# The first triangle stage of an attention-and-triangle kernel, written as a list of words over four steps and three blocks of fronts

## The chip, the cores and the metric

The kernel runs on one core of a Trainium2 chip. The metric is the device time of one execution in microseconds. Five executions of the kernel before gave a median of 3811.55 us, from 3808.18 to 3817.82. All arithmetic is in float32.

## What is computed

The input `x` has four images of 64 x 64 tokens with 256 channels. Two layers follow each other.

```python
# layer 0: attention over the 4096 tokens of an image
f = xt @ Wf + bf; g = xt @ Wg + bg; v = xt @ Wh + bh      # 32, 32 and 128 channels
beta = softmax(einsum('bqd,bkd->bqk', g, f), axis=-1)
x = x + (einsum('bqk,bkd->bqd', beta, v) @ Wo + bo)

# layer 1: triangle attention on the 64 x 64 grid, 8 heads of 32 channels
q, k, v1, v2 = (x @ W for W in (Wq, Wk, Wv1, Wv2))
att = softmax(einsum('bilhd,bljhd->biljh', q, k) / sqrt(32), axis=2)
out = einsum('biljh,bilhd,bljhd->bijhd', att, v1, v2)
h = layer_norm(x + out @ Wo)
y = layer_norm(h + relu(h @ W1 + b1) @ W2 + b2)
```

## The kernel before

**The stages.** For each of the four images there is a stage of layer 0 (attention, about 440 us) and a stage of the triangle product of layer 1 (`first_layer1` for image 0, `next_layer1` for the others). The rest of layer 1 (heads, norms and the two-layer perceptron, class `Tokens`) of image b runs inside the triangle stage of image b + 1, and that of the last image at the end. The triangle stage of image 0 has no such company. In its place it does the *fronts* of images 1 to 3 (class `Ahead`): for each of 24 blocks of 512 tokens it loads the tokens (`load`, the tile `xin`, one buffer of 512 KB), transposes them in two halves on TensorE (`turned`, L315), copies the halves out on ScalarE (`taken`, the tiles `xT`), multiplies them into values (`values`, `vp`) and into attention factors (`factors`, `gf`), and copies and stores all of it to DRAM, to be fetched back by `Ahead.fetch` before image 1's attention.

**One triangle step.** A stage has 32 steps, eight for each of four pairs of heads. A step treats eight rows i.

- `sums` (L758, L760, VectorE): the softmax's row sums of exponentials, and their reciprocals.
- `weights` (L768, ScalarE): eight scaled copies into `es`, two buffers.
- `turn_weights` (L785, TensorE) and `copy_weights` (L793, ScalarE): four transposes into the PSUM tile `att`, and a copy `attP` of the part that GpSimd needs, since it is given SBUF tiles.
- `stationary` (L812, ScalarE): v1 is written into a stationary matrix `wsel`, one for even and one for odd steps.
- `product` (L833): eight products of 128 x 2048 elements, `att` times `v2`. Of step 4i + 3 the last two, of the other steps the last three run on GpSimd (POOL) into `Rp`, which has two buffers; the others on VectorE (DVE) into `R`, three buffers. In four steps that makes 21 products on VectorE and 11 on GpSimd.
- `accumulate` (L843, TensorE): four matmuls for each product into one of the step's two PSUM tiles `acc`.
- `take` (L853, ScalarE), twice in a step: an `acc` is copied into `ao`, two buffers; `store` (L862): eight DMAs to DRAM.

The score blocks of the next pair of heads (`scores`, L731, and their two exponentials in `take_scores`, L741) are spread over the same steps, four blocks for each pair. `acc` and the score blocks share two PSUM buffers (`psA`); `tp`, `vp` and `gf` share two others (`psB`); `att` has two (`psC`). At the changes of pairs the stage loads q and k of the pair after next (`fetch_qk`, tile `qk`, one buffer, four DMAs of 512 KB) and v2 (`fetch_v2`, two buffers, two DMAs of 1 MB). All these loads, the tokens' and all stores of the stage are issued by one queue, SP's, in program order.

**What sets the order.** `run` is under `manual_schedule`: each engine gets its instructions in the order in which the Python code issues them, executes them in that order, and waits at each for the semaphores of what it needs. Before the change, `first_layer1` (L1152) is a loop over steps. The body issues one step's products and accumulates, the next step's `sums`, `weights`, `stationary` and `turn` among them, and in three steps of every four the parts of two blocks of fronts: the values and factors of the block before (`behind`) and the transposes and copies of this step's block (`forward`). `fetches` issues v2's loads at the start of a step, `fetch_qk` likewise; `ahead.load` stands right after the transposes that free `xin`.

`next_layer1` has another form already. A text, `ORDER`, lists words that stand for one piece of work each, and the code goes through the list once for a period of two steps. A number behind a slash says how many periods late a word is executed, so that one pass through the list mixes pieces of neighbouring periods.

Of the kernel before, what the change touches and what calls it, by code (L numbers as in the profile page):

```python
# [41 lines left out]
    r0/1 AO0/2 AO1/2 m1/1 RO4/2 RE5/1 SO/1 RO5/2 TO0/2 sp/1 AO4/2 AO6/2 r1/1 e0/1 e1/1 AO5/2 AE5/1 TO1/2  # L42
    RE4/1 AE4/1 z0/1 WO/1 RE3/1 VO/1 fi/2 SE z1/1 tO/1 so/1 RE6/1 RE0/1 cO/1 sa AE3/1 RE7/1 RE2/1 AE6/1
    AE2/1 AE0/1 rr/1 pp/1 WE RE1/1 AE7/1 AE1/1 fo/1 fa TE1/1 RO2/1 tE TE0/1 RO7/1 h1/-1 RO3/1 h0/-1 ht
    RO6/1 hU AO3/1 hT AO2/1 AO7/1 RO1/1 cE RO0/1 m0 VE
# [4 lines left out]
def attention_then_triangle_kernel(  # L50
# [171 lines left out]
    def factors(ps, xT, t):  # L222
        ps = ps.rearrange("p (w t) -> p w t", w=4)
        for w, wt in enumerate((wg_sb, wf_sb)):
            for cc in range(2):
                for n in range(4):
                    nc.tensor.matmul(
                        ps[32 * n : 32 * n + 32, w, :], wt[:, cc, :], xT[cc][:, ts(n, P)],
                        start=(cc == 0), stop=(cc == 1),
                    )  # L230
        for w, bias in enumerate((bias_g, bias_f)):
            nc.scalar.activation(t[:, w, 0:P], ps[:, w, :], AF.Identity, bias=bias)
# [16 lines left out]
    def front0(b):  # L249
# [22 lines left out]
        for q in range(8):  # L272
# [3 lines left out]
            factors(pb("gf"), [F.yT[cc][:, col] for cc in range(2)], gf)  # L276
# [22 lines left out]
    class Ahead:  # L299
        def __init__(self):  # L300
# [5 lines left out]
            self.n = 8 * (NB - 1)  # L306

# [7 lines left out]
        def turned(self, s):  # L315
            self.tp = []
            for cc in range(2):
                tp = pb("tp")
                for n in range(4):
                    nc.tensor.transpose(tp[:, ts(n, P)], self.x[:, n, ts(cc, P)], ident)  # L320
                self.tp.append(tp)

        def taken(self, s):
            self.xT = []
            for cc, tag in enumerate(("hT", "st")):
                t = work.tile([P, 512], F32, tag=tag, name="xT", bufs=2 + cc)
                self.xT.append(t)
                nc.scalar.copy(t, self.tp[cc])
                nc.sync.dma_start(out=self.d[1 + s // 8]["x"][ts(cc, P), ts(s % 8, 512)], in_=t)


        def values(self, s):
            self.vp = pb("vp")
            for n in range(4):
                for cc in range(2):
                    nc.tensor.matmul(
                        self.vp[:, ts(n, P)], self.xT[cc][:, ts(n, P)], wh_sb[:, cc, :],
                        start=(cc == 0), stop=(cc == 1),
                    )

        def valued(self, s):
            t = work.tile([P, 4, P], F32, tag="s4", name="va")
            nc.scalar.copy(t, self.vp.rearrange("p (n d) -> p n d", n=4))
            nc.sync.dma_start(out=self.d[1 + s // 8]["v"][:, s % 8 * 4 : s % 8 * 4 + 4, :], in_=t)

        def factors(self, s):
            t = work.tile([P, 2, C], F32, tag="h", name="gf", bufs=1)
            factors(pb("gf"), self.xT, t)
# [785 lines left out]
    def fetches(L, step):  # L1134
        pair, ig = divmod(step, NIG)
        L.fetch_v1(step + 2)
        if step == 2:
            L.fetch_v2(1)
        if ig == 0 and 0 < pair < NPAIR - 1:
            L.fetch_v2(pair + 1)  # L1140

    def first_layer1(L, ahead, F):
        b = 0
        ahead.load(0)
        waiting = behind = None
        for step in range(NSTEP):
            pair, ig = divmod(step, NIG)
            more = step + 1 < NSTEP  # L1150
            forward = step // 4 * 3 + step % 4 if step % 4 < 3 else None
            L.begin(step)  # L1152
            ahead.fetch(F, b + 1, step)
            k = L.npool(step)
            D_, Q_ = list(range(8 - k)), list(range(8 - k, 8))
            scored = step % 2 == 1 and pair + 1 < NPAIR
            if scored:
                L.take_scores()
            if step > 0:
                L.take(step - 1, 1)  # L1160
                L.store(step - 1)
            fetches(L, step)
            if scored and ig == 7 and pair + 2 < NPAIR:
                L.fetch_qk(pair + 2)

            late = scored and ig == NIG - 1

            def next_weights():
                if more:
                    L.sums(step + 1)  # L1170
                    L.weights(step + 1)

            L.product(step, Q_[0])
            L.product(step, D_[0])
            L.accumulate(step, D_[0])
            if behind is not None:
                ahead.values(behind)
            if not late:
                next_weights()
            if more:  # L1180
                L.stationary(step + 1)
            L.product(step, Q_[1])
            if behind is not None:
                ahead.valued(behind)
            L.accumulate(step, Q_[0])
            L.product(step, D_[1])
            L.accumulate(step, D_[1])
            if more and not late:
                L.turn(step + 1)
            if behind is not None:  # L1190
                ahead.factors(behind)
            L.product(step, D_[2])
            L.accumulate(step, D_[2])
            if forward is not None:
                ahead.turned(forward)
                ahead.load(forward + 1)
            if late:
                next_weights()
            if k == 3:
                L.product(step, Q_[2])  # L1200
            L.product(step, D_[3])
            L.accumulate(step, D_[3])
            L.take(step, 0)
            if forward is not None:
                ahead.taken(forward)
            behind = forward
            L.accumulate(step, Q_[1])

            if step % 2 == 0 and pair + 1 < NPAIR:
                L.scores(pair + 1, ig // 2)  # L1210
            if more and late:
                L.turn(step + 1)
            L.product(step, D_[4])
            if k == 3:
                L.accumulate(step, Q_[2])
            L.accumulate(step, D_[4])
            if k == 2:
                L.product(step, D_[5])
                L.accumulate(step, D_[5])
        ahead.fetch(F, b + 1, NSTEP)  # L1220
        L.take(NSTEP - 1, 1)
        L.store(NSTEP - 1)


    def next_layer1(b, L, rest, ahead, F):
        own = b == NB - 1
        t0 = NP * (b - 1)


        n2, n1, n0 = NP, NP + own, NP + 2 * own  # L1230
        made, added, taken, stored, held = {}, {}, {}, set(), []
        mv, rs, rn, mps, sps = {}, {}, {}, {}, {}

        def fetched(step):
            if F is not None and 24 <= step < 31:
                ahead.fetch(F, b + 1, step)
            if step == 2:
                L.fetch_v2(1)
            if step in (NIG, 2 * NIG):
                L.fetch_v2(step // NIG + 1)  # L1240


        def load(q, far=False):
            if q < NP or 24 + (q - NP) // 2 in stored:
                rest.load(t0 + q, far)
            else:
                held.append((q, far))

        def store(step):
            L.store(step)  # L1250
            stored.add(step)
            if own and step == 26:
                held.extend((NP + q, True) for q in (2, 3, 4))
            todo, held[:] = list(held), []
            for q, far in todo:
                load(q, far)

        def moments(q):
            if q not in mv:
                mv[q] = small.tile([P, 4, 2], F32, tag="mv", name="mv")  # L1260
            rest.mv = mv[q]

        def scores(j):
            L.scores(1 + j // 4, j % 4)
            sps[j] = L.sp
            if j % 4 == 3 and j // 4 + 2 < NPAIR:
                L.fetch_qk(j // 4 + 2)

        def of_step(word, i):
            step = 2 * i + "EO".index(word[1])  # L1270
            if not 0 <= step < NSTEP:
                return
            w = word[0]
            if w == "R":
# [3 lines left out]
                L.product(step, int(word[2]))  # L1278
                made[step] += 1
                if made[step] == 8:  # L1280
                    fetched(step + 1)
            elif w == "A":
                L.accumulate(step, int(word[2]))
            elif w == "T":
                L.take(step, int(word[2]))
                taken[step] = taken.get(step, 0) + 1
                if taken[step] == 2:
                    store(step)
# [11 lines left out]
            elif w == "c":  # L1300
                L.copy_weights(step)

# [54 lines left out]
        L.fetch_v1(2)  # L1357
        mps[1] = {}
        words = [(w.split("/") + ["0"])[:2] for w in ORDER]
        for period in range(NP + 4):  # L1360
            for word, late in words:
                i = period - int(late)
# [86 lines left out]
```

## Time and profile before

| | us |
|---|---|
| Median of five executions | 3811.55 |
| The profiled execution | 3809.94 |
| its span, from first to last instruction | 3808.1 |
| its first triangle stage, first to last product | 487.8 to 923.4 |
| 88 products on GpSimd in it, median of one | 4.588 |
| 168 products on VectorE in it, median of one | 2.280 |

In the profile, PE is TensorE, PEld its weight loads, DVE VectorE, ACT ScalarE, POOL GpSimd, and SPq the queue that issues DMAs. A row of the view by stretches gives, for each engine, the busy time in the stretch and the number of its instructions, then the TensorE clock that was granted (1 is full), the busy share of the DMA engines, and what they moved. A row of the timeline gives start, busy time, engine, line, operation, tiles written and read, and in brackets the idle time of the engine before it, with what ended that idle time. A matmul in float32 shows as two records, so an accumulate of four matmuls shows as eight. In the rows on DMA the last number is the median time from issue to landing.

### The profile page before, as it was taken

The numbers are of one execution on the slowest core, as the hardware profiler recorded it, in microseconds if no ns is written. First come the engines' busy times: TensorE is split into PE (matmuls) and PEld (weight loads), VectorE is DVE, ScalarE is ACT, GpSimd is POOL, SyncE is SP. The second block draws the span as 40 slices with busy tenths as digits, with TensorE's granted clock in tenths as the row PEclk, the third lists the DMA queues.
The fourth block names the chain that finished last, engine by engine and source line by source line (L and its number), as shares of the span: only waits on it lengthen the run. The fifth ranks groups of instructions, "written<-read, shape, count | busy, mean of one in ns | idle before, by whom it ended". The sixth has DMA issues, their size and how long they took to land.

```text
span 3808.1 us, 60145 instructions
## 1 busy us (share of the span) xinstructions
PE 3677.2 (97%) x23498; PEld 1795.3 (47%) x23498; DVE 2641.0 (69%) x2050; ACT 1934.1 (51%) x4257; POOL 1804.3 (47%) x930
## 2 busy tenths in 40 slices
PE   9999988888999999999999999999999999999997
PEld 5444444433444455554344445555344445555476
DVE  4444488897544459999544448999754455999976
ACT  3333355554333357776333346766533335677654
POOL 4000088896000049999100008999600004999954
PEclk9999999999999999999999999999999999999999
DMA  4111355544111164323111153343211116431221
GB/s 118 54 50 50 99 139 140 149 114 151 36 47 53 50 152 92 89 54 94 62 49 48 52 126 89 79 95 70 92 42 47 50 59 144 95 88 48 69 62 51
DMA packets 439750, 309.43 MB, mean 81 GB/s; under 512 B 299361, under 2 KB 404577, under 8 KB 432161
## 3 DMA queue, kind: packets, MB, share of 16 engines
q1 hardware_dynamic: 419952, 291.12, 29.0%
q10 hardware_dynamic: 16240, 8.59, 0.9%
q0 software_dynamic: 3264, 5.78, 0.6%
q8 instruction: 188, 3.08, 0.3%
q14 instruction: 106, 0.86, 0.1%
HBM read 165.88 MB, written 139.46 MB: 80 GB/s over the span
## 4 chain that ended last, share of the span: by engine, by line
PE 81%; POOL 7%; issue 3%; DVE 3%; DMA 3%; ACT 3%; SPq 0%; ACTq 0%; POOLq 0%; DVEq 0%
PE o L453 24%; PE acc L843 16%; PE proj L510 8%; PE s L431 7%; POOL Rp L833 6%; PE mp L1026 5%; PE zp L1046 5%; PE sp L731 3%; PE v1p L535 3%; PE hp L902 2%; PE y L495 1%; DVE R L833 1%; PE att L785 1%; ACT S L741 1%; PE den L470 1%
## 5 line engine op out<-in xcount | busy, mean ns | idle before, releaser
L833 POOL TENSOR_TENSOR Rp<-attP,v 128x2048 f32<-128x2048 f32 x328 | 1490.1, 4577 | 457.6 <-ACT attP L793 383.8
L833 DVE TENSOR_TENSOR R<-att,v 128x2048 f32<-128x2048 f32 x696 | 1548.4, 2273 | 109.0 <-PE acc L843 74.0
L460 DVE TENSOR_TENSOR esum<-esum,e 128x2048 f32<-128x2048 f32 x224 | 512.7, 2289 | 584.6 <-ACT e L442 581.5
L843 PE MATMUL acc<-R,wsel 128*32 128x512 f32 x5568 | 706.9, 602 | 42.4 <-DVE R L833 29.0
L442 ACT ACTIVATE e<-s 128x1024 f32<-128x1024 f32 x512 | 496.6, 1021 | 404.8 <-PE s L431 387.3
L954 POOL TENSOR_SCALAR nt<-mv 128x4 f32<-128x4 f32 (+1 forms) x51 | 9.8, 193 | 1283.2 <-DVE mv L919 1279.3
L453 PE MATMUL o<-e,vlo 128*128 128x512 f32 x1024 | 475.4, 607 | 0.0
L453 PE MATMUL o<-e,vhi 128*128 128x512 f32 x1024 | 472.6, 605 | 0.0
L853 ACT COPY ao<-acc 128x1024 f32<-128x1024 f32 x256 | 255.3, 1021 | 225.8 <-PE acc L843 196.6
L843 PE MATMUL acc<-Rp,wsel 128*32 128x512 f32 x2624 | 344.1, 598 | 23.8 <-POOL Rp L833 23.6
L843 PEld LDWEIGHTS acc<-R,wsel 128*32 128x32 f32 x5568 | 153.2, 110 | 377.5 <-issue 260.0
L453 PEld LDWEIGHTS o<-e,vlo 128*128 128x128 f32 x1024 | 184.6, 190 | 281.9 <-issue 281.9
L453 PEld LDWEIGHTS o<-e,vhi 128*128 128x128 f32 x1024 | 184.3, 189 | 279.6 <-issue 279.6
L431 PE MATMUL s<-gT,fT 32*128 32x512 f32 x2048 | 302.3, 640 | 4.3 <-ACT e L442 4.0
L768 ACT ACTIVATE es<-S,rd 128x64 f32<-128x64 f32 x1024 | 257.7, 335 | 11.0 <-DVE rd L760 7.7
L472 DVE RECIPROCAL rec<-den 128x512 f32<-128x512 f32 x32 | 107.4, 3357 | 215.6 <-PE den L470 215.6
L1046 PE MATMUL zp<-w,hid 128*128 128x256 f32 x1024 | 247.6, 387 | 7.2 <-ACT hid L1035 7.2
L1026 PE MATMUL mp<-hT,w 128*128 128x256 f32 x1024 | 249.5, 389 | 0.7 <-ACT hT L998 0.7
L1026 PEld LDWEIGHTS mp<-hT,w 128*128 128x128 f32 x1024 | 186.6, 190 | 101.4 <-ACT attP L793 36.0
L1046 PEld LDWEIGHTS zp<-w,hid 128*128 128x128 f32 x1024 | 186.4, 191 | 71.9 <-issue 31.9
L522 ACT COPY st<-proj 128x512 f32<-128x512 f32 x104 | 60.9, 585 | 293.2 <-issue 165.9
L843 PEld LDWEIGHTS acc<-Rp,wsel 128*32 128x32 f32 x2624 | 80.7, 110 | 212.4 <-issue 138.7
(166 smaller groups left out, 3820.7 us busy)
## 6 DMA issues: line engine op xcount, KB each, us to landing
v<-v2d SPq DMA_DIRECT2D x24, 1024.0 KB, 12.9
v1c<-v1d SPq DMA_DIRECT2D x128, 128.0 KB, 2.7
aT<-ao SPq DMA_DIRECT2D x1024, 16.0 KB, 1.9
A<-aT SPq DMA_DIRECT2D x256, 64.0 KB, 2.0
out_dram<-z SPq DMA_DIRECT2D x63, 256.0 KB, 2.5
y<-yT SPq DMA_DIRECT2D x56, 256.0 KB, 2.1
q<-st SPq DMA_DIRECT2D x56, 256.0 KB, 2.6
v1d<-st SPq DMA_DIRECT2D x56, 256.0 KB, 2.2
```

Source lines behind the costliest of these rows:

```text
L431: nc.tensor.matmul(s_ps[r // 2][:, r % 2, :], fT[rows, tt, ts(n, P)], gT[rows, ts(qb, QB)], start=True, stop=not safe,)
L442: nc.scalar.activation(e[g][:, 2 * j : 2 * j + 2, :], s_ps[j], AF.Exp)
L453: nc.tensor.matmul(o_ps[qb], F.v[tt][:, r * 4 + n, :], es[:, r, :], start=(k == 0 and r == 0), stop=(k == 7 and r == 3),)
L460: nc.vector.tensor_tensor(esum[qb], esum[qb], es, ALU.add)
L510: nc.tensor.matmul(ps, w[:, cc, rows], y(qb, cc), start=(cc == 0), stop=(cc == 1))
L535: nc.tensor.matmul(ps[:, ts(n, C)], y(qb, cc)[:, ts(m * 2 + n, P)], wv1_sb[:, cc, :], start=(cc == 0), stop=(cc == 1),)
L768: nc.scalar.mul(e[:, i, :], rows[:, i, :], rec[:, i : i + 1])
L833: eng.tensor_tensor(R, src.unsqueeze(1).to_broadcast([P, D, N]), v2[:, h], ALU.mult)
L843: nc.tensor.matmul(acc[32 * c : 32 * c + 32, n % 2, :], w[:, n, c, 16 * h : 16 * h + 32], R[:, ts(c, 8), :].rearrange("p d j -> p (d j)"), ...
L853: nc.scalar.copy(self.ao[step][:, ts(np, 2)].rearrange("p k d j -> p k (d j)"), self.acc[step][np])
L1026: nc.tensor.matmul(self.mp[:, fc % 2, :], w1_sb[:, cc, ts(fc, P)], self.hT[tt][:, cc, :], start=(cc == 0), stop=(cc == 1),)
L1046: nc.tensor.matmul(zp[:, n, :], self.hid[tt][:, fc, ts(n, P)], w2_sb[:, fc, :], start=(fc == 0), stop=(fc == 3 and tt not in self.hT2),)
```

## The change

The loop over steps is replaced by a second list of words, `ORDER0`, for a period of four steps and three blocks of fronts. The words of a step are now shared by both lists (`step_words`), so `ORDER`'s words have new names in the same order: the letter E or O, for an even or odd step, becomes 0 or 1. In `ORDER0` a word is a letter, a step (0 to 3) or block (0 to 2) of the period, and for some a last digit.

- `R23` is product 3 of step 2, `A23` its accumulate, `T20` and `T21` its two takes; after the second take the step is stored.
- `S`, `W`, `V`, `t`, `c` are sums, weights, stationary (and the load of v1 two steps on), transposes of the weights, and the copy `attP`.
- `sp0` and `sp1` are blocks of scores, `e01`, `e00`, `e11`, `e10` their exponentials by halves. The fourth block of a pair is followed by `fetch_qk` at once, if a pair is left to load.
- `P01`, `P00` are the transposes of block 0's halves 1 and 0, `C01`, `C00` their copies and stores; after a block's second `P` the next block's tokens are loaded.
- `v`, `u` are values and their copy and store; `g`, `a` are factors and their copy (bias) and store.
- `/1` is one period late, `/-1` one early.

`fetch_v2` is now issued when the eighth product of step 1, 7 or 15 has been issued. `Ahead.turned` and `Ahead.taken` do one half at a time, and factors and their bias are two functions, so that other words can stand between.

```diff
+ORDER0 = """
+    A22/1 t3/1 R23/1 V3/1 W0 A26/1 A21/1 g2/1 A23/1 A25/1 R24/1 T20/1 sp1/1 A24/1 S2 S3 c3/1 t0 R27/1
+    v1/1 R31/1 R33/1 a2/1 A27/1 e11/1 e10/1 R30/1 A33/1 A31/1 R32/1 v2/1 u1/1 R37/1 P01 T21/1 A37/1
+    A30/1 C01 S1 R35/1 c0 R36/1 A32/1 R34/1 P00 A35/1 A36/1 C00 g0 V0 R01 A34/1 u2/1 T30/1 R00 W1 R05
+    T31/1 A05 R06 v0 A00 A01 V1 R03 R02 A03 t1 a0 c1 R04 u0 A06 R13 P11 R07 P10 A02 A07 R15 W2 R12 A04
+    T00 C11 T01 sp0 R16 t2 e01 R10 c2 A12 P21 e00 R11 C10 S0/-1 A15 W3 A13 A16 C21 P20 A10 R17 R14 V2
+    A11 A14 A17 R26 g1 R25 R20 T11 T10 a1 R22 R21 A20 C20
+""".split()
...
-        def turned(self, s):
-            self.tp = []
-            for cc in range(2):
-                tp = pb("tp")
-                for n in range(4):
-                    nc.tensor.transpose(tp[:, ts(n, P)], self.x[:, n, ts(cc, P)], ident)
-                self.tp.append(tp)
+        def turned(self, s, cc):
+            tp = self.tp[s, cc] = pb("tp")
+            for n in range(4):
+                nc.tensor.transpose(tp[:, ts(n, P)], self.x[:, n, ts(cc, P)], ident)
...
+    def step_words(L, fetched, stored):
+        made, taken, sps = {}, {}, {}
+
+        def do(w, step, m):
             if not 0 <= step < NSTEP:
                 return
             if w == "R":
                 if step not in made:
                     made[step] = 0
                     L.begin(step)
-                L.product(step, int(word[2]))
+                L.product(step, m)
                 made[step] += 1
                 if made[step] == 8:
+                    if step == 1:
+                        L.fetch_v2(1)
+                    if step in (NIG - 1, 2 * NIG - 1):
+                        L.fetch_v2((step + 1) // NIG + 1)
                     fetched(step + 1)
...
+        def scores(j):
+            if j == 1:
+                scores(0)
+                L.take_scores()
+            if 0 <= j < 12:
+                L.scores(1 + j // 4, j % 4)
+                sps[j] = L.sp
+                if j % 4 == 3 and j // 4 + 2 < NPAIR:
+                    L.fetch_qk(j // 4 + 2)
...
+        def front_word(w, s, cc):
+            if not 0 <= s < ahead.n:
+                return
+            if w == "P":
+                ahead.turned(s, cc)
+                turned[s] = turned.get(s, 0) + 1
+                if turned[s] == 2:
+                    ahead.load(s + 1)
+                    if s + 1 == ahead.n:
+                        ahead.fetch(F, 1, 31)
...
+        for period in range(NSTEP // 4 + 3):
+            for word, late in words_of(ORDER0):
+                i, last = period - late, int(word[-1])
+                if word[0:2] == "sp":
+                    if i >= 0:
+                        scores(2 * i + 1 + last)
+                elif word[0] == "e":
+                    if i >= 0:
+                        take_scores(2 * i + 1 + int(word[1]), last)
+                elif word[0] in "RATSWVtc":
+                    step_word(word[0], 4 * i + int(word[1]), last)
+                else:
+                    front_word(word[0], 3 * i + int(word[1]), last)
```

## The prediction

> **What bounds the kernel now.** I read the page first (TensorE busy for 97% of the span), then the busy times in stretches, because the change touches one stage only: the first triangle stage, from its first product at 487.8 us to its last at 923.4.
>
> ```profile
> core 0: us, PE busy (x) PEld busy (x) DVE busy (x) ACT busy (x) POOL busy (x), PEclk, DMA share, GB/s
> 487.84:921.20 433.36, 381.29 (x4263) 175.47 (x4262) 394.60 (x230) 236.81 (x614) 399.32 (x88) 0.98 0.51 140
> ```
> ```profile
> 518.02:570.53 52.51, 48.15 (x572) 22.58 (x568) 49.63 (x30) 31.04 (x81) 49.99 (x12) 1.00 0.53 143
> 570.53:629.94 59.41, 50.14 (x572) 23.57 (x568) 50.85 (x31) 31.00 (x81) 49.88 (x11) 0.94 0.65 163
> 629.94:682.52 52.58, 48.15 (x572) 22.55 (x568) 48.63 (x29) 30.98 (x80) 49.94 (x12) 1.00 0.36 104
> ...
> 820.86:870.74 49.88, 41.64 (x424) 18.57 (x420) 47.43 (x28) 26.29 (x74) 49.88 (x12) 1.00 0.55 141
> ```
>
> A row is one period of four steps (11 POOL and 21 DVE products). POOL does 399.3 us of work in 433.4; a period needs at least 49.88 on POOL (last row: 11 products without a gap, 4.53 each) and 21 x 2.19 + 4 x 0.83 = 49.3 on DVE (five products and a pair of sums end to end take 11.78, from 876.10 to 887.88). It takes 52.5 undisturbed and 59.4 and 59.8 twice. So the stage is bound by the two product engines, and only their idle time can be won. Next, POOL's own order of time:
>
> ```profile
> 503.23 13.65 POOL L833 TENSOR_TENSOR Rp<-attP,v 128x2048 f32<-128x2048 f32 x3 [1.85 <-PE acc L843]
> 518.02 36.34 POOL L833 TENSOR_TENSOR Rp<-attP,v 128x2048 f32<-128x2048 f32 x8 [1.15 <-PE acc L843]
> ...
> 596.46 27.17 POOL L833 TENSOR_TENSOR Rp<-attP,v 128x2048 f32<-128x2048 f32 x6 [3.22 <-PE att L785]
> 629.94 36.27 POOL L833 TENSOR_TENSOR Rp<-attP,v 128x2048 f32<-128x2048 f32 x8 [6.31 <-ACT ao L853]
> ...
> 820.86 63.46 POOL L833 TENSOR_TENSOR Rp<-attP,v 128x2048 f32<-128x2048 f32 x14 [3.19 <-PE att L785]
> ```
>
> The bracket is the idle time. All of them sum to 34.0: start 1.85 + 1.15; around 600-630 3.22 + 6.31, and the same again (3.26 + 6.67) around 710-742; 3.19 at 820.86; the other seven 8.4. Last, what ended the long ones:
>
> ```profile
> 624.91 1.94 PE L320 MATMUL tp<-ident,xin 128*128 128x128 f32 x8 [4.96 <-DMA xin<-in_x_dram]
> ...
> 626.78 1.94 PE L843 MATMUL acc<-R,wsel 128*32 128x512 f32 x8
> ```
> ```profile
> 611.34 1.42 SPq L311 DMA_DIRECT2D xin<-in_x_dram  x1
> ```
> ```profile
> xin<-in_x_dram SPq DMA_DIRECT2D x21, 512.0 KB, 4.1
> v<-v2d SPq DMA_DIRECT2D x6, 1024.0 KB, 10.8
> ```
>
> A tokens' load lands 4.1 us after its issue; issued behind the two 1 MB loads of v2 (610.1) it took 13.4, and PE, which works in order, stood 4.96 us, then ran slowly (eight transposes 1.94 instead of 1.02, one accumulate 1.71 start to start instead of 0.87).
>
> **The change part by part.** Engine by engine the two programs have the same instructions in the same number, and differ in order only within this stage (and in the branch with maxima, which doesn't run). The later triangle stages get the same words under other names: cost zero. So the sum is POOL's and DVE's idle time.
>
> *Taken away.* All 34.0 us of POOL's idle time, and the 2.2 that DVE works on after POOL ends (921.2 to 923.4): 36.2.
>
> *Steady period.* I laid the words of one period end to end, from R23/1, with row durations: DVE product 2.24, sums pair 0.87, POOL product 4.6, accumulate 0.87, block of scores 2.0, turning weights 0.59, half a front's transposes 0.52, values 1.98, factors 0.95, ACT 1.02 (take, half of scores), 2.0 (weights), 1.0 (wsel). PE has 32 x 0.87 + 2 x 2.0 + 4 x 0.59 + 3 x (1.04 + 1.98 + 0.95) = 46.1 of 50; ACT 31; SP's issues 4 x (5.0 + 0.6) + 3 x 2.45 = 29.8. Each buffer is met in time: R32 starts at 13.0 and waits for A33, done at 11.6; R12 at 34.0 for A02 (31.5). The tightest are POOL's, with two buffers: R05 must not start before A37 ends (15.9), which puts R27 2.1 to 2.6 us after R23, and nothing contradicts it. So a period near POOL's 49.9 fits. Ends: 0 idle, and 2.65 (the period stays 52.55). I take 0.5, nearest to the next stage, already driven by such words, where the limiting PE is busy 27.76 of 27.76 us per two steps. Six periods with scores: 3.0.
>
> *The qk loads.* Issued after the fourth block of scores (sp0 in periods 1 and 3), now behind the load of tokens needed next, and 24 us ahead of the following one; cover 24 against 7.4 to 9 us of landing: zero. Without that cover they would do what v2 does.
>
> *The v2 loads.* R34/1 completes a step and issues the next pair's v2; the buffer's last reader is R34 itself, so SP waits to 20.6 in the period. P00, the next word, issues the tokens that P11 needs. They go out at 21.8, land 13.4 later, 35.2; P11 stands on PE at 30.1. **This wait stays**: 5.1 us. Behind P11: P10 (both 1.94, slow), A02 (1.7), and R12 on DVE waits for A02's buffer until 38.8 instead of 34.0; then sp0, t2 and A12 (44.2), for whose buffer R11 is 5.8 late; A15 frees POOL's R17 6.6 late. I take 6 a time, 12 for two. Ends: 0 (tokens land in the 9.5 us from P00 to P11), and 7.2 (59.8 less 52.6, today's price).
>
> The Trainium skill ("TensorE: Matmul & The Clock Gate", Part 1) has the array at half clock after an idle window of about 3.4 us, for about as long again. By it the slow phase would cost up to 1.7 us a time, against about 2.0 from the rows above; the sum would be 0.6 lower.
>
> *Start.* Before, the first accumulates wait for products only. Now P01, P00 and g0 stand ahead of A05 on PE. Their tokens are issued at 482.98; a transfer issued 0.07 us earlier landed after 10.72, so P01 begins near 493.7. P01 and P00 1.94, copy 0.6, g0 1.9, A05 1.7 (slow clock: 0.83 in 480-500): about 500. R07 on POOL waits for A05's buffer from 497.0: 3.1. A06 now stands behind v0 and three accumulates (506.9), so R15 waits 2.3 more. Sum 5.4, between 3.0 (as before) and 7. Period 0 also does two blocks of scores at sp0, 2.0 on PE ahead of A12: I take 1.0 of it.
>
> *Last two periods.* The loads of gT, vlo and yT (0.5 to 1 MB) are issued at R34 and R07, a word before tokens again: 1.5, between 0 and 5.
>
> *End.* R36 ends POOL's work; R34, DVE's last, ends 4.5 later: 4.5.
>
> New idle: 3.0 + 12 + 5.4 + 1.0 + 1.5 + 4.5 = 27.4. Gain 36.2 - 27.4 = 8.8. The profiled execution took 3809.9 (span 3808.1), so 3801.1; the median of five is 1.6 above it: **3803**.
>
> **The rivals.**
> 1. *The v2 wait is hidden too.* For it: tokens land in 4.1 us without company, and PE has 4 us a period to spare. Against: 13.4 in the same succession. 12 less: 3791.
> 2. *The period stays at 52.5.* For it: R05 has half a microsecond between two constraints, and 33 of DVE's waits (34.2 us) are for accumulates. Against: PE has slack in the walk. 6 x 2.15 = 12.9 more: 3816.
> 3. *Slower: the single gf buffer.* a1 writes it at 47.7 of a period, and a2 may write it again at 4.6 of the next; between them lie eight stores (5.0 us of SP) and gf's own landing, 2.2. ACT's a2 then starts at about 5.0; e11, e10 stand behind it, their buffer holds A33 (10.8), and A33 holds DVE's R32. ACT has 2.8 us in hand. If gf lands more than 2.8 us later than that, each further microsecond is paid in all eight periods. It passes the forecast's gain at 1.1, and is 0.2% slower at 2.1. At 3: 24 more, 3827.
> 4. *The order isn't what the words say.* The instruction order shows it is: 3812, almost no chance.
>
> **How the numbers follow.** About 0.2% (7.6 us, from 3804 to 3819) is what a measurement can tell from no change. Forecast 0.42 (3797 to 3809; 0.27 of it faster, 0.15 within), rival 1 0.25 (faster), rival 2 0.18 (0.15 within, 0.03 slower), rival 3 0.13 (slower), rival 4 0.02 (within). Faster 0.52, within 0.32, slower 0.16. The range takes in rivals 1 and 2: 3787 to 3817; rival 3 and little else is left out.
>
> **What would show it.** Right: POOL in runs of ten products and more, periods of 50 to 51 us except two of about 56, and in these PE waiting some 5 us for xin near P11. Rival 1: no such wait. Rival 2: POOL waits of 1 to 3 us for accumulates in every period. Rival 3: ACT's gf waiting for a DMA (ahg, ahf), and scores' copies late behind it. Wrong altogether if the end of the stage moves by other than the total, or if the later stages change length.

## The result, and the profile after

| | before | after |
|---|---|---|
| Median beside each other, us | 3812.01 (46 runs) | 3809.64 (25 runs) |
| Ratio of the times, 95% interval | | 0.9993 (0.9987 to 0.9998) |
| Profiled execution's span, us | 3808.1 | 3810.0 |
| First triangle stage, first to last product, us | 435.6 | 433.2 |
| POOL's idle time in it, us | 34.0 | 31.2 |
| DVE's work after POOL's end, us | 2.2 | 2.15 |

The change made the kernel 2.4 us faster, 0.07%, which is within the 0.2% called no change. The time lies in the predicted range (3787 to 3817) and 6.6 us above the forecast of 3803. The profiled execution of after is longer than that of before although its stage is shorter: its first triangle product starts at 489.98 instead of 487.84, behind code that did not change. Over all ten profiled executions here this start lies between 487.8 and 490.0, so below the length of the stage is compared, not the time at which it ends. What follows the stage took 2884.7 us before and 2886.8 after (2881.4 to 2889.9 over the ten), so a difference of medians can be some microseconds off the stage's.

The lines of after's program stand 16 further down (the product is L849, the accumulate L859, the transposes of tokens L336). First the row of the stage in the view by stretches:

```profile
core 0: us, PE busy (x) PEld busy (x) DVE busy (x) ACT busy (x) POOL busy (x), PEclk, DMA share, GB/s
489.98:923.17 433.19, 387.12 (x4280) 177.97 (x4278) 392.93 (x224) 234.25 (x615) 399.56 (x88) 0.96 0.52 141
```

POOL's work is nearly the same, 399.6 us against 399.3, so the new length is told by its idle time. POOL's own order of time in after; the bracket is the idle time ahead of a run of products:

```profile
490.02 8.99 POOL L849 TENSOR_TENSOR Rp<-attP,v 128x2048 f32<-128x2048 f32 x2 [327.48 <-ACT attP L809]
503.92 4.55 POOL L849 TENSOR_TENSOR Rp<-attP,v 128x2048 f32<-128x2048 f32 x1 [4.90 <-PE acc L859]
510.39 9.12 POOL L849 TENSOR_TENSOR Rp<-attP,v 128x2048 f32<-128x2048 f32 x2 [1.92 <-PE acc L859]
521.29 27.20 POOL L849 TENSOR_TENSOR Rp<-attP,v 128x2048 f32<-128x2048 f32 x6 [1.79 <-PE acc L859]
551.02 22.76 POOL L849 TENSOR_TENSOR Rp<-attP,v 128x2048 f32<-128x2048 f32 x5 [2.53 <-PE acc L859]
574.24 45.56 POOL L849 TENSOR_TENSOR Rp<-attP,v 128x2048 f32<-128x2048 f32 x10 [0.46 <-PE acc L859]
624.77 4.58 POOL L849 TENSOR_TENSOR Rp<-attP,v 128x2048 f32<-128x2048 f32 x1 [4.97 <-PE acc L859]
631.02 95.43 POOL L849 TENSOR_TENSOR Rp<-attP,v 128x2048 f32<-128x2048 f32 x21 [1.67 <-PE acc L859]
730.84 4.57 POOL L849 TENSOR_TENSOR Rp<-attP,v 128x2048 f32<-128x2048 f32 x1 [4.39 <-PE acc L859]
737.22 99.89 POOL L849 TENSOR_TENSOR Rp<-attP,v 128x2048 f32<-128x2048 f32 x22 [1.82 <-PE acc L859]
839.33 27.21 POOL L849 TENSOR_TENSOR Rp<-attP,v 128x2048 f32<-128x2048 f32 x6 [2.22 <-PE acc L859]
866.90 22.70 POOL L849 TENSOR_TENSOR Rp<-attP,v 128x2048 f32<-128x2048 f32 x5 [0.36 <-PE acc L859]
893.76 27.26 POOL L849 TENSOR_TENSOR Rp<-attP,v 128x2048 f32<-128x2048 f32 x6 [4.17 <-PE acc L859]
```

Two things are to be seen. Left to itself, the list keeps POOL at its limit: 21 products and then 22 without a gap, 95.43 and 99.89 us, 4.54 us each, where before had a gap of 1 us or more after every 3 to 8 products, but for one run of 14 (its gap is 0.59). And all that is left of idle time sits in a few places, each ended "by PE's accumulate", which names the last link only. The link ahead of it is on PE and on SP's queue. Around 620 us in after, SP's issues and then what PE does:

```profile
604.77 1.12 SPq L730 DMA_DIRECT2D v<-v2d  x2
605.98 0.53 SPq L329 DMA_DIRECT2D xin<-in_x_dram  x1
...
612.48 9.96 SPq L878 DMA_DIRECT2D aT<-ao  x8
```
```profile
619.98 1.94 PE L336 MATMUL tp<-ident,xin 128*128 128x128 f32 x8 [5.55 <-DMA xin<-in_x_dram]
621.86 1.87 PE L859 MATMUL acc<-R,wsel 128*32 128x512 f32 x8
623.55 1.03 PE L859 MATMUL acc<-Rp,wsel 128*32 128x512 f32 x8
```

The tokens are issued right behind the two 1 MB loads of v2 and let PE begin 14.0 us later; PE stands 5.55 us with every accumulate queued behind. This is the wait that the prediction said would stay. The next ones it had at zero or small. Around 543 us, ACT, and the stores on SP's queue ahead of it:

```profile
523.90 1.22 SPq L730 DMA_DIRECT2D v<-v2d  x2
...
529.03 10.83 SPq L878 DMA_DIRECT2D aT<-ao  x8
...
540.59 1.08 SPq L366 DMA_DIRECT2D ahf<-gf  x1
```
```profile
542.99 0.37 ACT L247 ACTIVATE gf<-gf,bias_g 128x128 f32<-128x128 f32 x1 [7.13 <-DMA ahf<-gf]
```

Eight stores of a step, 5.0 us of SP in undisturbed steps, take 10.83 behind v2; gf's own stores stand behind them; ACT cannot write the one gf buffer until they have landed. And near the end, where the loads for image 1's attention are mixed in:

```profile
828.84 0.42 SPq L252 DMA_DIRECT2D gT<-ahg  x1
829.36 0.64 SPq L329 DMA_DIRECT2D xin<-in_x_dram  x1
```
```profile
836.20 1.08 PE L336 MATMUL tp<-ident,xin 128*128 128x128 f32 x4 [2.89 <-DMA xin<-in_x_dram]
837.22 1.94 PE L859 MATMUL acc<-Rp,wsel 128*32 128x512 f32 x8
```

With the load of gT issued half a microsecond ahead, PE can begin on the tokens 6.8 us after their issue, where a tokens' load by itself landed after 4.1.

### The profile page after: what moved, and what is told of

Read it like the earlier page. It is cut to its first block, busy times and chain, and to the rows that moved or that the text cites. A ratio compares the mean times of both kernels' runs of the same rounds, so it can differ in the third digit from the quotient of the medians.

```text
span 3810.0 us, 60208 instructions
## 1 busy us (share of the span) xinstructions
PE 3685.2 (97%) x23498; PEld 1798.4 (47%) x23498; DVE 2639.5 (69%) x2050; ACT 1932.3 (51%) x4257; POOL 1805.2 (47%) x930
## 4 chain that ended last, share of the span: by engine, by line
PE 79%; POOL 5%; DVE 4%; DMA 4%; issue 4%; ACT 2%; SPq 1%; ACTq 0%; DVEq 0%; POOLq 0%
PE o L469 24%; PE acc L859 16%; PE proj L526 8%; PE s L447 7%; PE mp L1042 5%; PE zp L1062 5%; POOL Rp L849 4%; PE v1p L551 3%; PE sp L747 3%; DVE R L849 3%; PE hp L918 2%; DMA xin<-in_x_dram 2%; PE y L511 2%; PE att L801 1%; PE den L486 1%
## 5 line engine op out<-in xcount | busy, mean ns | idle before, releaser
L849 POOL TENSOR_TENSOR Rp<-attP,v 128x2048 f32<-128x2048 f32 x328 | 1490.5, 4579 | 456.2 <-ACT attP L809 385.0
L849 DVE TENSOR_TENSOR R<-att,v 128x2048 f32<-128x2048 f32 x696 | 1546.4, 2274 | 107.3 <-PE acc L859 76.0
L859 PE MATMUL acc<-R,wsel 128*32 128x512 f32 x5568 | 705.4, 605 | 33.8 <-DVE R L849 22.9
L859 PE MATMUL acc<-Rp,wsel 128*32 128x512 f32 x2624 | 349.9, 605 | 13.2 <-POOL Rp L849 12.4
L859 PEld LDWEIGHTS acc<-R,wsel 128*32 128x32 f32 x5568 | 153.1, 110 | 366.5 <-issue 267.3
L859 PEld LDWEIGHTS acc<-Rp,wsel 128*32 128x32 f32 x2624 | 80.9, 111 | 202.0 <-issue 139.0
```

The lines of the kernel that those rows point to most:

```text
L849: eng.tensor_tensor(R, src.unsqueeze(1).to_broadcast([P, D, N]), v2[:, h], ALU.mult)
L859: nc.tensor.matmul(acc[32 * c : 32 * c + 32, n % 2, :], w[:, n, c, 16 * h : 16 * h + 32], R[:, ts(c, 8), :].rearrange("p d j -> p (d j)"), ...
```

## The experiments

The theory after this reading (A): the list reaches the limit of the two product engines, and what is left is tokens, and stores, that queue behind larger loads on SP's queue. The rival (B): the list's order itself is at its limit, and a wait that is taken away comes back at the next buffer. The table has all runs; the stage is measured from first to last product, the idle time is POOL's in it, and the fourth column is PE's waiting time for `xin` (in how many waits).

| run | median, us | ratio to before (95%) | stage, us | POOL idle, us | PE for xin, us |
|---|---|---|---|---|---|
| after | 3809.64 | 0.9993 (0.9987 to 0.9998) | 433.2 | 31.2 | 24.2 (8) |
| e1 | 3798.65 | 0.9953 (0.9939 to 0.9967) | 423.6 | 22.1 | 20.4 (8) |
| e2 | 3804.52 | 0.9976 (0.9967 to 0.9986) | 427.6 | 25.9 | 14.5 (7) |
| e3 | 3783.15 | 0.9921 (0.9906 to 0.9936) | 409.3 | 9.6 | 6.3 (1) |
| e4 | 3801.61 | 0.9962 (0.9948 to 0.9975) | 423.7 | 22.0 | none |
| e5 | 3792.31 | 0.9938 (0.9924 to 0.9951) | 410.9 | 10.5 | 13.0 (7) |
| e6 | 3783.40 | 0.9912 (0.9897 to 0.9927) | 404.4 | 3.7 | 5.9 (6) |
| e7 | 3808.00 | 0.9980 (0.9971 to 0.9989) | 424.7 | 23.5 | 18.8 (7) |
| e8 | 3796.88 | 0.9948 (0.9935 to 0.9962) | 417.1 | 15.6 | 16.7 (8) |

e1 to e4 ran on one chip, on which before took 3813.48, and e5 to e8 on another, 3816.31; between the two groups the ratios are compared.

**e1: v2 a step later.** The next pair's v2 is issued behind the eighth product of steps 2, 10 and 18 instead of 1, 7 and 15, in the first triangle stage alone, so that the tokens needed soon go ahead of it.

```diff
-    def step_words(L, fetched, stored):
+    def step_words(L, fetched, stored, v2_at=(1, NIG - 1, 2 * NIG - 1)):
...
-                    if step == 1:
-                        L.fetch_v2(1)
-                    if step in (NIG - 1, 2 * NIG - 1):
-                        L.fetch_v2((step + 1) // NIG + 1)
+                    if step in v2_at:
+                        L.fetch_v2(v2_at.index(step) + 1)
...
-        step_word, scores, take_scores = step_words(L, fetched, lambda step: None)
+        step_word, scores, take_scores = step_words(L, fetched, lambda step: None, (2, 10, 18))
```

> The changed kernel, with the loads of v2 issued when the eighth product of step 2, 10 or 18 has been issued (R24/1, early in a period, after which the next tokens' load is 14 us away) instead of step 1, 7 or 15. Everything else as in the changed kernel. Theory A (the idle time that is left in the stage comes from tokens that queue behind larger loads): the two waits of 5.6 us for xin go, with the 6.6 and 6.2 us of POOL's idle time behind them, and the gf wait of period 1 (2.5 us of POOL) too: 13 to 15 us less than the changed kernel's 3809.6, about 3796. Theory B (the list's order is at its limit, and the wait moves to another buffer): POOL idles elsewhere by as much, 3807 to 3812.

The ratio falls by 0.0040, some 15 us, more than the 9.1 us that POOL's idle time loses and the 9.6 us by which the stage is shorter; the intervals of the two ratios allow for that difference. POOL's idle time of 4.97 + 1.67 and 4.39 + 1.82 us is gone, and so is that of period 1, as these rows of e1's POOL show:

```profile
519.60 49.97 POOL L849 TENSOR_TENSOR Rp<-attP,v 128x2048 f32<-128x2048 f32 x11 [1.76 <-PE acc L859]
569.86 27.23 POOL L849 TENSOR_TENSOR Rp<-attP,v 128x2048 f32<-128x2048 f32 x6 [0.29 <-PE acc L859]
597.66 72.69 POOL L849 TENSOR_TENSOR Rp<-attP,v 128x2048 f32<-128x2048 f32 x16 [0.58 <-ACT attP L809]
671.86 27.22 POOL L849 TENSOR_TENSOR Rp<-attP,v 128x2048 f32<-128x2048 f32 x6 [1.50 <-PE acc L859]
```

A holds for the waits behind v2. Not all of the time was won, though: the gaps of 1.50 us here and of 2.09 at 774 are new. They stand a period later than the old ones, where after had none, behind waits of PE for tokens (2.31 and 2.72 us) that have no large load right ahead of them on the queue. The last two periods lost 1.5 us more than in after.

**e2: v2 after steps 1, 9 and 17.** The same edit with (1, 9, 17). v2 is clear of the tokens here too, but stands ahead of gf's stores.

> The changed kernel, with the loads of v2 issued after the eighth product of step 1, 9 or 17 (R14, late in a period, right after the tokens' load and right ahead of eight stores and of the stores of gf). Theory A with the single gf buffer as a second queue: the token waits go (13 us of POOL), but in each of the two periods after a load ACT waits some 7 us for gf's stores, as it did once in the changed kernel at 536 to 543, and POOL 2.5 to 3 us behind it: 7 to 8 us less than the changed kernel, about 3802. If gf's buffer does not matter: 13 less, 3797. Theory B: no gain, 3810.

PE waits less for tokens than in e1 (14.5 us against 20.4), and yet the kernel is slower than e1. POOL in e2, and ACT ahead of its first long gap:

```profile
653.12 22.76 POOL L849 TENSOR_TENSOR Rp<-attP,v 128x2048 f32<-128x2048 f32 x5 [4.20 <-PE acc L859]
...
758.62 45.47 POOL L849 TENSOR_TENSOR Rp<-attP,v 128x2048 f32<-128x2048 f32 x10 [4.48 <-PE acc L859]
```
```profile
643.47 0.37 ACT L247 ACTIVATE gf<-gf,bias_g 128x128 f32<-128x128 f32 x1 [7.32 <-DMA ahf<-gf]
```

This is the single gf buffer, the mechanism of the prediction's third rival, in the periods in which v2 delays gf's stores. The gaps are larger than the 2.5 to 3 us expected, and the gain is smaller for it.

**e8: e2 with two gf buffers.** One edit to e2, which shows whether that reading is right.

```diff
-            t = work.tile([P, 2, C], F32, tag="h", name="gf", bufs=1)
+            t = work.tile([P, 2, P], F32, tag="gf2", name="gf", bufs=2)
```

> The kernel with v2's loads after steps 1, 9 and 17 (3804.5 in its run, POOL idle 4.20 us at 653 and 4.48 at 759), and the factors' tile gf in two buffers instead of one, nothing else. If the single gf buffer is the mechanism of these two waits (ACT's gf behind the landing of the stores of the gf before, which stand behind v2 on SP's queue), both go, 8 to 9 us, POOL's idle time falls from 25.9 to about 17, and the median is 3795 to 3797. If the wait only passes to the next thing behind the same queue (ao's two buffers, the tokens), POOL still stands 3 to 4 us at each of the two places and the median stays at 3802 to 3805.

POOL in e8, over the same stretch:

```profile
569.35 99.94 POOL L849 TENSOR_TENSOR Rp<-attP,v 128x2048 f32<-128x2048 f32 x22 [0.53 <-PE acc L859]
669.70 77.16 POOL L849 TENSOR_TENSOR Rp<-attP,v 128x2048 f32<-128x2048 f32 x17 [0.42 <-PE acc L859]
```

Both gaps are gone, ACT no longer waits for gf's stores at all, POOL's idle time falls by 10.3 us and the ratio by 0.0028 (10.7 us). The wait did not pass on to the next buffer. The mechanism is shown. The edit also takes gf out of a tag that it shares with a tile of later stages; what follows the stage took 2886.4 us against 2887.2 in e2, so the gain lies in the stage.

**e3: the tokens loaded once.** Only the first block of tokens is loaded; the other 23 loads are left out, and the fronts are computed from the first block's tokens again.

```diff
         def load(self, s):
-            if s < self.n:
+            if s == 0:
```

> The changed kernel with the tokens of the fronts loaded once: the 23 further loads are left out, and all 24 blocks of fronts work on the first block's tokens (so the values and factors of images 1 to 3 are not those of the reference). All other work stays. Theory A: nothing but the first xin wait is left; POOL loses its 12.9 us at the v2 loads and most of the 6.8 us in the last two periods, 15 to 20 us less, 3790 to 3795. Theory B: POOL's waits for accumulates stay, less than 5 us gained.

The stage falls to 409.3 us, and the median is 7 us below the lower end expected. Apart from the start, POOL has one gap of 0.77 us and then works 77 products in one run of 349.42 us. The missing loads (11.5 MB) also took most of POOL's gap behind gf in period 1 (2.53 to 0.77), which the expectation had kept, and all of those in the last two periods. So none of these waits belongs to the order of the list alone: they need the loads. This run takes the loads away altogether; that their places on the queue are what counts is shown by e1, e5 and e6.

**e4: the loop of before, with two of its v2 loads moved.** In the kernel before, the v2 loads of pairs 2 and 3 go out at the start of steps 11 and 19 instead of 8 and 16.

```diff
-        if ig == 0 and 0 < pair < NPAIR - 1:
-            L.fetch_v2(pair + 1)
+        if step in (11, 19):
+            L.fetch_v2(pair + 1)
```

> The kernel before, with no list of words; only the loads of v2 of pairs 2 and 3 are issued at the start of steps 11 and 19 instead of 8 and 16, that is in the one step of four in which no tokens are loaded. Theory A: the two waits for xin of about 5 us, with POOL's 6.3 and 6.7, go there as well; 12 to 14 us less than the kernel before, about 3799, and so more than the list of words itself brought. Theory B (the loop's order is the limit, and the list was needed): less than 4 us.

One moved line in the old loop gives 0.38%, five times what the whole list gave. No wait of PE for `xin` is left in its stage; what remains is put down here to the old order, though ACT still waits 7.0 us there for stores. Rows of e4's POOL:

```profile
597.24 27.20 POOL L833 TENSOR_TENSOR Rp<-attP,v 128x2048 f32<-128x2048 f32 x6 [3.22 <-PE att L785]
624.91 36.30 POOL L833 TENSOR_TENSOR Rp<-attP,v 128x2048 f32<-128x2048 f32 x8 [0.46 <-PE acc L843]
662.71 13.67 POOL L833 TENSOR_TENSOR Rp<-attP,v 128x2048 f32<-128x2048 f32 x3 [1.51 <-PE acc L843]
677.42 22.76 POOL L833 TENSOR_TENSOR Rp<-attP,v 128x2048 f32<-128x2048 f32 x5 [1.04 <-PE acc L843]
703.43 27.21 POOL L833 TENSOR_TENSOR Rp<-attP,v 128x2048 f32<-128x2048 f32 x6 [3.25 <-PE att L785]
```

The same pattern comes back every 106 us: 3.2, 0.5, 1.5 and 1.0.

**e5: e1 with the late loads regrouped.** The loads for image 1's attention leave the places ahead of a token load (fetch 31, which the front words issue, stays as it was).

```diff
-            if 24 <= step < 31:
-                ahead.fetch(F, 1, step)
+            for n in {23: (28,), 26: (24, 25), 27: (26, 27, 29), 31: (30,)}.get(step, ()):
+                ahead.fetch(F, 1, n)
```

> The changed kernel with v2's loads after steps 2, 10 and 18 (as in the run before that gave 3798.65), and in its last two periods the loads of gT, vlo and yT for the next stage issued so that none of them stands ahead of a load of tokens that is needed in the next 12 us: one after step 23, two after step 26, three after step 27, one after step 31, instead of one after each of the steps 24 to 30. Theory A (what idle time is left comes of tokens that queue behind larger loads on SP's queue): the 2.82, 0.57 and 4.89 us of POOL's idle time after 820 us, 8.3 in all, go but for 1 to 2, and the median is 3791 to 3793. Theory B (the list's own order has reached its limit at the end, because the last fronts and the last steps are left without company): POOL stands as long as before at 827 and 882 us, and the median stays at 3798 to 3799.

Of the 8.3 us of idle time after 820 us, 0.93 is left; A holds. The stage is shorter by 12.7 us, though, because the 1.50 and 2.09 us of e1 in its middle are missing too, and these the edit does not touch. POOL in e5 from 599 us on:

```profile
599.05 272.46 POOL L849 TENSOR_TENSOR Rp<-attP,v 128x2048 f32<-128x2048 f32 x60 [0.44 <-ACT attP L809]
872.44 27.29 POOL L849 TENSOR_TENSOR Rp<-attP,v 128x2048 f32<-128x2048 f32 x6 [0.93 <-PE acc L859]
```

So some 4 us of the difference between the two profiles do not come of the edit (what brings them is told below, under the hardware); by the ratio e5 is 0.0015 below e1, with intervals of 0.0014 either way.

**e6: e5 with the first tokens earlier.** The first block's load is issued in image 0's attention, behind the first pair's v2, instead of behind q, k and v2 at the start of the stage.

```diff
     # layer0, where the first pair's v2 is fetched
+        if b == 0:
+            ahead.load(0)
     # first_layer1
-        ahead.load(0)
```

> The run above with one more edit: the first block of tokens is loaded while image 0's attention still runs, right after the first pair's v2, instead of at the start of the triangle stage behind its q, k and v2. Theory A: at the start DVE and POOL stood because PE, in order, waited for these tokens; POOL's 5.04 and most of 2.02 and 1.76 us at the start go, 5 to 7 us, and the median is 3785 to 3788. Theory B (the start costs what it costs because the list puts transposes, factors and values of the first block ahead of the first accumulates, whether or not the tokens are there): the wait of 6.2 us for tokens goes, POOL's idle time at the start falls by 2 us or less, and the median is 3789 to 3792.

The idle time at the start falls by 7.7 us (5.20 + 1.84 + 2.09 to 1.44), and the median is below the expected one. The stage and POOL of e6:

```profile
489.43:893.78 404.35, 379.42 (x4279) 174.01 (x4278) 392.29 (x224) 234.79 (x615) 399.64 (x88) 0.99 0.56 150
```
```profile
489.43 22.66 POOL L851 TENSOR_TENSOR Rp<-attP,v 128x2048 f32<-128x2048 f32 x5 [327.62 <-DMA qk<-k]
513.53 177.30 POOL L851 TENSOR_TENSOR Rp<-attP,v 128x2048 f32<-128x2048 f32 x39 [1.44 <-PE acc L861]
691.07 72.69 POOL L851 TENSOR_TENSOR Rp<-attP,v 128x2048 f32<-128x2048 f32 x16 [0.24 <-POOL Rp L851]
764.09 27.24 POOL L851 TENSOR_TENSOR Rp<-attP,v 128x2048 f32<-128x2048 f32 x6 [0.33 <-PE acc L861]
791.72 22.71 POOL L851 TENSOR_TENSOR Rp<-attP,v 128x2048 f32<-128x2048 f32 x5 [0.40 <-POOL Rp L851]
815.51 49.93 POOL L851 TENSOR_TENSOR Rp<-attP,v 128x2048 f32<-128x2048 f32 x11 [1.08 <-PE acc L861]
865.68 27.28 POOL L851 TENSOR_TENSOR Rp<-attP,v 128x2048 f32<-128x2048 f32 x6 [0.23 <-PE acc L861]
```

POOL is busy for 399.6 of 404.4 us: the stage stands at the limit of its two product engines. e6 is 0.9% faster than before and the fastest version that computes all of it. Between e4, the old loop without a wait for tokens, and e6 lie 19.3 us of stage and 0.0050 of the ratio (19 us): that is what the list's order is worth once the transfers are out of its way, as far as one profile of each and intervals of 0.0013 and 0.0015 on the ratios tell.

**e7: after with the first tokens earlier, and nothing else.** Only the edit of e6.

> The changed kernel with nothing edited but the load of the first block of tokens, issued while image 0's attention still runs. Theory A: the start's 8.6 us of POOL's idle time fall by 5 to 7, nothing later moves, and the median is 3803 to 3805. Theory B (the list's words ahead of the first accumulates cost the time): a fall by 2 us or less, 3807 to 3809.

The three gaps of the start, 8.6 us, become one of 1.28, and the stage is 8.5 us shorter (1.8 of the gain lies in the last periods). The median is above the expected one on a chip where before was 4.8 us above its first median; by the ratio the gain over after is 0.0013, 5 us, with intervals of 0.0006 and 0.0009 either way. A's size is confirmed by the trace, by the median only in its direction.

## Why the prediction was right in range and short in its forecast

The way of the sum was right: POOL's idle time and DVE's end account for the stage, and the engines' work did not change. The sum of new idle time was 27.4 and became 33.35 (31.2 + 2.15), so that of 8.8 us of gain 2.85 are left by this ledger; POOL's products took 0.24 longer in all, and the stage shows 2.4. The prediction gave 0.52 to a gain that can be told from no change and 0.32 to none that can, half of that for rival 2; none it was, and not by rival 2. Term by term, predicted and measured:

| step | predicted, us | measured, us |
|---|---|---|
| steady period | 3.0 | 0.5 |
| v2 loads, "This wait stays" | 12 | 12.85 |
| start, with period 0's scores | 6.4 | 8.6 |
| single gf buffer | 0 | 2.5 |
| last two periods | 1.5 | 6.75 |
| end | 4.5 | 2.15 |

**Right: the steady period, a little better than said.** The walk through the words had no idle time, and there was almost none (0.46 us, behind a wait of 1.34 for tokens at 572); e6 has 39 products in a row. Rival 2 (a period of 52.5) falls.

**Right: the v2 wait.** 4.97 + 1.67 and 4.39 + 1.82 us of POOL; PE stood 5.55 and 5.24 at P11, where 5.1 was said. Rival 1 falls. The slow phase behind the wait cost 1.7 us (eight transposes 1.88 from start to start instead of 1.02, one accumulate 1.69 instead of 0.87), where the prediction read about 2.0 from its rows. e1 shows that the wait came of the place of two issues: moved by some words, v2 delays no tokens.

**Wrong in size: "The loads of gT, vlo and yT (0.5 to 1 MB) are issued at R34 and R07, a word before tokens again: 1.5".** It measured 6.75, the largest miss, beyond the stated end of 5. The mechanism is the one of the v2 step, and the sum used it there and took only part of it here. Behind such a load PE could begin 6.8 and 7.3 us after the tokens' issue instead of 4.1, stood 2.89 and 2.39 us, and then ran slowly (accumulates 1.70 from start to start; at the second it was slow already before the wait). e5 takes it away with nothing but other places for the loads.

**Wrong in size: the start.** P01 was to begin 5.9 us after the first product and began 7.5 after (the tokens took 12.3 us behind the four 512 KB loads of q and k, not 10.72). The chain behind it, PE slow and R07 waiting, came as said, with 4.90 for 3.1. e6 and e7 show that nearly all of it was the load's place: 1.44 and 1.28 us are left.

**Wrong: rival 3 as it was put, not its mechanism.** The gf buffer was to cost nothing, or something in all eight periods. ACT did wait for gf's stores eight times (23.3 us), but only the longest, 7.13, reached POOL, with 2.53. "ACT has 2.8 us in hand" was too little: in after itself the waits of 4.82 and 4.95 behind the qk loads left POOL without a gap, and in e6 waits of up to 5.1 us left it with gaps of about a microsecond at most. What the prediction missed is that v2, issued once in period 1 ahead of a step's stores, stretches these stores from 5.0 to 10.8 us, so gf's buffer costs POOL time in one period and not in all.

**Too dear: the end**, 2.15 for 4.5. With the steady period it took back 4.9 of the 10.8 us by which the other terms were short. So that the total missed by only 6 us is in part luck: errors of both signs met.

So the list did what it says, and its gain went to one queue. POOL's idle time can be parted, roughly, by the two runs in which the loads are out of the way: of the 34.0 us of before, 22.0 stay in e4 and are the old order's own, and 12.0 were v2's; of the 31.2 of after, 3.7 stay in e6 and are the list's own, and 27.5 were SP's queue. The list took away 18.3 and brought 15.5: at the start, at the gf buffer and at the two late loads, where the old order's PE did not wait for a load.

## What to carry to other kernels

A new order of work moves its DMA issues as well: for each load that the in-order engine needs within some ten microseconds, list what stands ahead of it on its queue and add those bytes to its landing time, for small loads as for the large. When a reordering gives little, see what ends each idle time two links back: here every gap read "PE's accumulate", and the cause was mostly a load's place on SP's queue, which moving a few issues cured. Keep the order and the places of the transfers apart when judging either; each hid the other's gain here.

## What the runs showed of the hardware

A stall of PE above some length costs more than itself. Up to 780 us e1 and e5 execute the same instructions, on two chips, and the same tokens landed at slightly different moments. PE in e1, then in e5:

```profile
669.17 0.66 PE L336 MATMUL tp<-ident,xin 128*128 128x128 f32 x4 [2.31 <-DMA xin<-in_x_dram]
669.75 1.93 PE L859 MATMUL acc<-Rp,wsel 128*32 128x512 f32 x8
671.46 1.88 PE L859 MATMUL acc<-R,wsel 128*32 128x512 f32 x8
673.16 1.03 PE L859 MATMUL acc<-Rp,wsel 128*32 128x512 f32 x8
```
```profile
669.77 0.66 PE L336 MATMUL tp<-ident,xin 128*128 128x128 f32 x4 [1.52 <-DMA xin<-in_x_dram]
670.36 1.06 PE L859 MATMUL acc<-Rp,wsel 128*32 128x512 f32 x8
671.24 1.04 PE L859 MATMUL acc<-R,wsel 128*32 128x512 f32 x8
```

After 2.31 us two accumulates took 1.71 each from start to start, after 1.52 us 0.88, and the granted clock was 0.50 from 669.75 to 673.16 in e1 and 1.00 from 669.77 to 673.16 in e5; POOL then stood 1.50 us in e1 and not at all in e5. In the ten profiles every wait for tokens of 1.87 us and more was followed by slow matmuls, and those up to 1.83 us by fast ones, except in the last two periods, where PE had stood for a product shortly before and a wait of 1.48 (e5, at 869 us) or 0.45 (e6, at 863) was enough. Waits for other engines show that this is no sharp limit: PE ran fast after 2.12 us (before, at 835) and slowly after 1.91 (e6, at 811). The Trainium skill ("TensorE: Matmul & The Clock Gate", Part 1) explains such slow stretches by a clock gate that halves the array's clock after an idle window of about 3.4 us, in windows that run freely. The slow stretch here lasted 3.41 us (669.75 to 673.16), and 3.57 us in after (619.98 to 623.55), which agrees; but it followed 2.31 us of standing, and in e6 one followed 1.91, less than the window that the page gives.

Large loads delayed the issue of small stores. Eight stores of 16 KB, 5.0 us of SP in an undisturbed step, took 10.83, 9.96 and 10.14 us behind 2 MB of v2 and 9.09 and 9.02 behind 2 MB of q and k (all in after), so that all issues after them, the small ones too, went out 4 to 6 us later.
